# A gated cross-attention and expert kernel: the transposes of the second LayerNorm's input move from TensorE to VectorE blocks and DMAs, with four smaller edits

## The chip, the cores and the metric

The kernel runs on one core of one Trainium2 chip. Its time is the device time of one execution in microseconds; the metric is the median of the runs. Lower is better.

## What is computed

x is 2 x 1024 x 2048 in f32, the context 2 x 2048 x 2048. Cut to what matters:

```python
def fake_quant(x, scale, zp):                  # QMIN 0, QMAX 255
    q = clip(round(x / scale + zp), 0, 255)
    return (q - zp) * scale

x = x + tanh(g_xattn) * (fake_quant(layernorm(x)) @ fake_quant(ctx))
y = layernorm(x)
logits = y @ route_w.T                         # 8 experts
weight = one_hot(argmax(logits)) * max(logits)
h = einsum("bsd,erd->bser", y, A)              # 8 experts x rank 16
x = x + tanh(g_ffn) * einsum("bser,eor->bso", weight * h, Bw)
```

The first step's matmul (1024 x 2048 x 2048 for each of two batches) is the large one. In the text, "x2" is x after that first step, the input of the second LayerNorm.

## The kernel before, in words

**Tiles.** The tokens are 16 tiles of 128 rows (8 per batch). The context of a batch is 4 strips of 512 columns; a strip is loaded in 4 quarters ("st", 1 MB each), scaled to integers by ScalarE (line 347), clamped by VectorE (line 351) and kept as f16 ("q"). A tile of x is normalized and quantized by ScalarE (line 471) after statistics from VectorE (line 435) and a power on GpSimd (line 459), and is then transposed: by TensorE for tiles 0 to 3 (line 493), by a transposing DMA for the others (line 484). The product of tile t and strip s is a group of 16 matmuls into one PSUM bank (line 529, "mm").

**After a group.** VectorE adds c times the product to x in place (line 538), then adds r and corr (line 543). r is a number per row from the sum of the tile's quantized values (line 505, on ScalarE); corr is a row over all columns, from the column sums of the quantized context (line 366 for batch 0: matmuls with ones; line 377 and following for batch 1: VectorE adds first, then one matmul), both because the quantized values are kept centred on 128. Line 543 also gives the row sums of x2.

**The second step, "ffn", of a tile.** x2 is transposed by TensorE in 16 pieces of 128 x 128 ("px", line 569), ScalarE copies them to SBUF ("xnt", line 583), and 16 products with the 136 columns of A and route_w ("hl", line 576; an f32 matmul is two instructions here) follow. The mean has been taken off the weights once (line 314 and following), so hl needs x2 itself only. The variance comes from a ScalarE pass (line 601). VectorE picks the expert (lines 612 to 621), wh is transposed ("pw", line 633) and multiplied with Bw ("po", line 646, 8 instructions), and VectorE adds the result (line 654). GpSimd's queue stores the tile (line 667); the last tile is stored by SP in four pieces.

**What sets the order.** A planner at build time (class Plan) gives every task an engine, a cost, a rank, the tasks it needs and the buffers it takes. It walks through time and lets each free engine take its first ready task by rank; the instructions are then written out in that order, one stream per engine, and each engine runs its own stream strictly in order. TensorE's, ScalarE's, VectorE's, GpSimd's and SP's orders are all fixed in this way. SP issues the loads and the transposing DMAs. The planner also models DMA: a rate and a delay. Tiles are grouped into sets that share a pass over the strips: [0, 1, 2, 3], [4], [5, 6, 7], [8, 9, 10], then one by one. Buffers have fixed numbers by kind: 6 for x, 3 for st, 4 for q2 and so on; a load waits until its buffer is free. [...]

**The start.** ScalarE's queue loads six scalars, each spread to 128 partitions (line 251); SP loads x in four pieces for tile 0 (line 419), then st and x in turns.

Of the kernel before, what the change touches and what calls it, by code (L numbers as in the profile page):

```python
# [9 lines left out]
F32 = mybir.dt.float32  # L10
F16 = mybir.dt.float16
I16 = mybir.dt.int16
U8 = mybir.dt.uint8
# [30 lines left out]
class Plan:  # L44
# [4 lines left out]
    def __init__(self, units, banks, hop, dma_rate, dma_delay):  # L49
        self.units = units  # L50
        self.banks = banks
        self.hop, self.rate, self.delay = hop, dma_rate, dma_delay
        self.tasks = []
# [19 lines left out]
    def walk(self):  # L73
        free = {k: list(range(n)) for k, n in self.units.items()}
        free_banks = list(range(8))
        in_use = {k: 0 for k in self.banks}
# [12 lines left out]
        def room(t):  # L89
            want = {}  # L90
            for b in t.bufs:
                if b.unit is None:
                    want[b.kind] = want.get(b.kind, 0) + 1
            n_banks = 0
            for k, n in want.items():
                if k in self.banks:
                    n_banks += n
                    if in_use[k] + n > self.banks[k]:
                        return False
                elif len(free[k]) < n:  # L100
                    return False
            return n_banks <= len(free_banks)

        while any(waiting.values()):
            for r in [r for r in releases if r[0] <= now]:
                releases.remove(r)
                b = r[1]
                if b.kind in self.banks:
                    in_use[b.kind] -= 1
                    free_banks.append(b.unit)  # L110
                else:
                    free[b.kind].append(b.unit)
            nxt = []
            for eng, w in waiting.items():
# [19 lines left out]
                for b in pick.bufs:  # L134
                    if b.unit is None:
                        if b.kind in self.banks:
                            in_use[b.kind] += 1
                            b.unit = free_banks.pop(0)
                        else:
                            b.unit = free[b.kind].pop(0)  # L140
# [23 lines left out]
def flamingo_gated_kernel(  # L164
# [39 lines left out]
    NT = B * MT  # L204

    TURN = set(range(4, NT))
    units = {"x": 6, "st": 3, "q2": 4, "q1": 2, "q1t": 5, "xnt": 3, "wh": 2, "wht": 2, "sum": 1,
             "bn": 3, "sel": 2}
    banks = {"mm": 4, "tp": 2, "hl": 1, "po": 2, "cs": 1}
    plan = Plan(units, banks, hop=0.15, dma_rate=300e3, dma_delay=2.0)  # L210
# [9 lines left out]
    def buf(kind, name, shape, dt):  # L220
        if kind in banks:
            return Buf(kind, lambda u: psum.tile(shape, dt, tag=f"bank{u}", name=name))
        return Buf(kind, lambda u: work.tile(shape, dt, tag=f"{kind}{u}", name=name))
# [11 lines left out]
    junk = const.tile([P, D], U8, name="junk")  # L235
# [12 lines left out]

    def load_scalars():
        for i, a in enumerate((x1_scale, x1_zp, x2_scale, x2_zp, g_xattn, g_ffn)):  # L250
            nc.scalar.dma_start(raw[:, i : i + 1], a.partition_broadcast(P))

    def set_up():
        make_identity(nc, idh)
        make_identity(nc, idf)
        nc.gpsimd.memset(mhalf, -0.5)
        nc.gpsimd.memset(ones, 1.0)
        nc.gpsimd.memset(dmean, 1.0 / D)
        for e in range(E):
            nc.gpsimd.memset(order8[:, e : e + 1], float(E - e))  # L260

    def scalars():
        nc.vector.reciprocal(rs1, s1)
        nc.vector.reciprocal(rs2, s2)
# [13 lines left out]
    sets = [[0, 1, 2, 3], [4], [5, 6, 7], [8, 9, 10]] + [[t] for t in range(11, NT)]  # L278
# [5 lines left out]
    for tiles in sets:  # L284
# [10 lines left out]
    t_raw = add(ACT, 3.0, -100, load_scalars, nbytes=1)  # L295
    t_set = add(POOL, 3.0, -100, set_up)
    t_rs = add(DVE, 0.4, -50, scalars, needs=[t_raw])
    t_th = add(
        ACT, 1.5, 0.5, lambda: nc.scalar.activation(th, raw[:, 4:6], AF.Tanh), needs=[t_raw]
    )  # L300
    t_sc = add(DVE, 1.2, 0.5, gates, needs=[t_th])
    def weights(after):
# [15 lines left out]
        def subtract():  # L318
            nc.vector.tensor_tensor(
                war, war, mw.unsqueeze(1).to_broadcast([P, KC, ER + E]), ALU.subtract  # L320
            )

        a = add(PE, 4.0, 13.7, means, [t_war, t_set], [pm])
        b = add(DVE, 0.3, 13.7, lambda: nc.vector.tensor_copy(mw, pm.ap()[:, : ER + E]), [a], [pm])
        return add(DVE, 2.3, 13.7, subtract, [b]), t_wb
# [5 lines left out]
    def strip(b, s):  # L331
# [5 lines left out]
        for q in range(NQ):  # L337
            st = buf("st", f"st_{b}_{s}_{q}", [P, QK, NC], F32)
            rank = i - 4 + q * len(tiles) / NQ

            def load(q=q, st=st):
                rows = cx[b, q * QK * P : (q + 1) * QK * P, ts(s, NC)]
                nc.sync.dma_start(st.ap(), rows.rearrange("(k p) n -> p k n", p=P))

            def scale(q=q, st=st):
                part = qb.ap()[:, ts(q, QK), :]
                nc.scalar.activation(part.bitcast(I16), st.ap(), AF.Relu, bias=z2, scale=rs2)  # L347
# [5 lines left out]
            a = t_ctx[b, s, q] = add(SP, 0.6, rank, load, [], [st], nbytes=4 * P * QK * NC)  # L353
# [6 lines left out]
        if b == 0:  # L360
# [10 lines left out]
        else:  # L371
            tb = buf("sum", f"sum_{b}_{s}", [P, 4, NC], F16)

            def add_up(j):
                t, v = tb.ap(), qb.ap()
# [9 lines left out]
            for j in range(4):  # L385
# [6 lines left out]
                lambda: nc.tensor.matmul(cs.ap(), ones, tb.ap()[:, 0, :], start=True, stop=True),  # L392
# [10 lines left out]

    xb, q1t, t_x, t_q1t, t_r, rs_, t_pre, acc_sums = {}, {}, {}, {}, {}, {}, [], {}

    def tokens(t):
# [8 lines left out]
        for i in range(pieces):  # L415
            loads.append(
                add(
                    SP, 0.6, {1: -4.5, 2: -2.9, 3: -1.9}.get(t, rank - 4),
                    lambda i=i: nc.sync.dma_start(
# [6 lines left out]
        bn = buf("bn", f"bn_{t}", [P, NN, 6], F32)  # L426
        mv = small.tile([P, 2], F32, name=f"mv_{t}")
        wk = small.tile([P, 8], F32, name=f"wk_{t}")
        y, u, v, a, nb, rw, r, ve = (wk[:, i : i + 1] for i in range(8))
        mean, var = mv[:, 0:1], mv[:, 1:2]  # L430

        stats = [
            add(
                DVE, 0.68, rank,
                lambda n=n: nc.vector.bn_stats(bn.ap()[:, n, :], xx.ap()[:, ts(n, NC)]),  # L435
                [loads[n * pieces // NN]], [xx, bn],
            )
            for n in range(NN)
        ]

        def scale():
# [6 lines left out]
            nc.vector.scalar_tensor_tensor(v, mean, a, z1, ALU.mult, ALU.subtract)  # L448
            nc.vector.tensor_scalar(nb, v, -1.0, None, ALU.mult)  # L449

        
        def variance():
            nc.vector.bn_aggr(mv, bn.ap())
            nc.vector.tensor_scalar(ve, var, EPS, None, ALU.add)  # L454

        ag = add(DVE, 0.45, rank, variance, stats, [bn])
# [5 lines left out]
        qb = buf("q1", f"q1_{t}", [P, D], F16)  # L462
# [3 lines left out]
        t_q1t[t] = []  # L466
        clamps = []
        for h in range(H):
# [11 lines left out]
            clamps.append(add(DVE, 0.7 / H, rank, clamp, [d], [qb]))  # L480
        if t in TURN:
# [5 lines left out]
            t_q1t[t] = [a_] * (KC // 8)  # L487
        for h in range(0 if t in TURN else KC // 8):
            pt = buf("tp", f"pq_{t}_{h}", [P, 8, P], F16)

            def turn(h=h, pt=pt):
                for j in range(8):
                    nc.tensor.transpose(pt.ap()[:, j, :], qb.ap()[:, ts(8 * h + j, P)], idh)  # L493

            a_ = add(PE, 0.65, rank, turn, [clamps[h * H // 2], t_set], [qb, pt])
            t_q1t[t].append(
                add(
                    ACT, 1.01, rank,
                    lambda h=h, pt=pt: nc.scalar.copy(qt.ap()[:, ts(h, 8), :], pt.ap()),
# [4 lines left out]
        def row_sum():  # L504
            nc.scalar.activation(junk, qb.ap(), AF.Copy, accum_out=rw)  # L505

        d = add(ACT, 2.12, first[t] + 0.5, row_sum, clamps, [qb])
# [4 lines left out]
        acc_sums[t] = small.tile([P, NN], F32, name=f"ss_{t}")  # L512
# [5 lines left out]
    t_x2, t_mm = {}, {}  # L518

    def group(t, s):  # L520
# [5 lines left out]
        for k in range(KC):  # L526
            p = add(
                PE, 0.221, whole[t, s] + k / 100,
# [6 lines left out]
        xs = lambda: xx.ap()[:, ts(s, NC)]  # L535
        e = add(
            DVE, 0.76, i,
            lambda: nc.vector.scalar_tensor_tensor(xs(), acc.ap(), c, xs(), ALU.mult, ALU.add),  # L538
            [p, t_sc] + t_x[t], [acc, xx],
# [4 lines left out]
                xs(), xs(), rs_[t], corr[:, ts(s, NC)], ALU.add, ALU.add,  # L544
                accum_out=acc_sums[t][:, s : s + 1],
# [8 lines left out]
    def ffn(t):  # L554
        b, m = divmod(t, MT)
        end = t == NT - 1
        rank = last[t] + 1.2
        xx = xb[t]
        fs = small.tile([P, 8], F32, name=f"fs_{t}")
        nm, sq, v, r2 = (fs[:, i : i + 1] for i in range(4))  # L560
        hl = buf("hl", f"hl_{t}", [P, NC], F32)
        p = None
        for n in range(NN):
            pt = buf("tp", f"px_{t}_{n}", [P, NC], F32)
            xn = buf("xnt", f"xnt_{t}_{n}", [P, NC], F32)
# [7 lines left out]
            def product(n=n, xn=xn):  # L573
                for j in range(BPC):
                    k = n * BPC + j
                    nc.tensor.matmul(  # L576
                        hl.ap()[:, : ER + E], xn.ap()[:, ts(j, P)], war[:, k, :],
# [3 lines left out]
            a = add(PE, 0.55, rank - 0.1, turn, [t_x2[t, n], t_set], [xx, pt])  # L581
            d = add(
                ACT, 0.6, rank - 0.2, lambda pt=pt, xn=xn: nc.scalar.copy(xn.ap(), pt.ap()),  # L583
                [a], [pt, xn],
            )
            p = add(PE, 1.13, rank, product, [d, t_wc] + ([p] if p else []), [xn, hl])
# [6 lines left out]
        def inverse():  # L593
# [7 lines left out]
            lambda: nc.scalar.activation(junk, xx.ap(), AF.Square, bias=nm, accum_out=sq),  # L601
            [a], [xx],
# [3 lines left out]
        top = small.tile([P, 3], F32, name=f"top_{t}")  # L606
# [35 lines left out]
        for n in range(NN):  # L642
            po = buf("po", f"po_{t}_{n}", [P, NC], F32)
            a = add(
                PE, 0.93, rank,
# [80 lines left out]
```

## Time and profile before

| | |
|---|---|
| Median of 3 runs | 430.47 us (429.17 to 432.62) |
| The profiled execution | 428.93 us |
| Its span in the profile | 427.2 us |
| TensorE busy | 394.6 us (92%) |
| VectorE busy | 278.7 us (65%) |
| ScalarE busy | 212.6 us (50%) |
| Moved by DMA | 75.92 MB, mean 178 GB/s |
| TensorE clock granted | full in every slice |

All durations in this document come from one profiled execution. A row of the page's groups reads: line, engine, operation, out<-in with the tile names, shapes, count, then busy us and mean ns of one, then the idle time just before these instructions and what ended most of it. Matmuls overlap in the trace, so a mean ns of a matmul is longer than the time that it adds to a stream; the chain of waits, whose pieces do not overlap, shows that time. A name with q after the engine (SPq) is its sequencer, which issues DMAs.

### The profile page before, as it was taken

To read this page: it belongs to the slowest core of one execution; us is meant where nothing else is said; L and a number is where in the kernel's file an instruction comes from. 1 tells how busy PE (TensorE), PEld (TensorE's weight loads), DVE (VectorE), ACT (ScalarE), POOL (GpSimd) and SP (SyncE) were. 2 spreads that over 40 slices of the span, in tenths; PEclk is the share of its full clock that TensorE was granted. 3 is DMA by queue.
4 is the path that set the end of the run, shared out by engine and by line. 5 is a ranking of instruction groups with operands and counts; after the bars stand their busy time and mean duration, and the time that the engine had idled before them with its cause. 6 is when DMAs were issued, how large, how long until landed. Compare 5 with 4: busy or idle time off the path is not lost.

```text
span 427.2 us, 5486 instructions
## 1 busy us (share of the span) xinstructions
PE 394.6 (92%) x2100; PEld 228.9 (54%) x2100; DVE 278.7 (65%) x703; ACT 212.6 (50%) x211; POOL 22.0 (5%) x50
## 2 busy tenths in 40 slices
PE   0278999999999899999999999999999999999994
PEld 0134444447767446444765644477647474746561
DVE  2774744497555897996744899897588635354433
ACT  1699984438723457773895522368108230303030
POOL 1100000010000100100000010000101000000000
PEclk9999999999999999999999999999999999999999
DMA  4995889964016784999739654022475402010022
GB/s 130 404 351 199 290 297 359 404 236 93 2 61 235 233 265 142 335 303 394 170 96 350 257 201 114 12 38 49 139 269 136 148 2 98 2 61 38 9 91 98
DMA packets 50426, 75.92 MB, mean 178 GB/s; under 512 B 26976, under 2 KB 29024, under 8 KB 46432
## 3 DMA queue, kind: packets, MB, share of 16 engines
q1 hardware_dynamic: 47376, 59.84, 44.4%
q0 software_dynamic: 2160, 15.73, 8.9%
q8 instruction: 16, 0.26, 0.2%
q10 hardware_dynamic: 864, 0.00, 0.1%
q14 instruction: 10, 0.08, 0.1%
HBM read 52.50 MB, written 16.78 MB: 162 GB/s over the span
## 4 chain that ended last, share of the span: by engine, by line
PE 60%; issue 11%; DVE 10%; ACT 10%; DMA 7%; POOL 1%; ACTq 0%; SPq 0%; POOLq 0%
PE mm L529 40%; PE po L646 9%; PE hl L576 6%; DMA x<-in_x_dram 3%; DVE bn L435 3%; ACT q L347 3%; DMA st<-in_ctx_dram 3%; PE px L569 2%; ACT q L471 2%; PE cs L366 2%; ACT junk L601 2%; DVE x L543 1%; ACT xnt L583 1%; ACT junk L505 1%; DVE x L538 1%
## 5 line engine op out<-in xcount | busy, mean ns | idle before, releaser
L529 PE MATMUL mm<-q,q1t 128*128 128x512 f16 x1024 | 233.7, 380 | 6.7 <-DVE q L351 4.0
L529 PEld LDWEIGHTS <-q1t 128*128 128x128 f16 x1024 | 100.2, 98 | 125.2 <-issue 13.6
L347 ACT ACTIVATE q<-st,raw,rs 128x2048 int16<-128x2048 f32 x32 | 66.2, 2093 | 21.0 <-DMA st<-in_ctx_dram 18.7
L538 DVE SCALAR_TENSOR_TENSOR x<-mm,sc,x 128x512 f32<-128x512 f32 x64 | 46.5, 747 | 32.4 <-PE mm L529 32.0
L576 PE MATMUL hl<-war,xnt 128*128 128x136 f32 x512 | 65.5, 281 | 1.4 <-ACT xnt L583 1.1
L576 PEld LDWEIGHTS hl<-war,xnt 128*128 128x128 f32 x512 | 62.2, 190 | 7.1 <-ACT xnt L583 3.3
L646 PE MATMUL po<-wb,wht 128*128 128x512 f32 x128 | 61.3, 598 | 0.4 <-ACT wht L639 0.4
L654 DVE SCALAR_TENSOR_TENSOR x<-po,th,x 128x512 f32<-128x512 f32 x64 | 47.0, 748 | 21.1 <-PE po L646 19.2
L583 ACT COPY xnt<-px 128x512 f32<-128x512 f32 x64 | 35.4, 582 | 47.1 <-PE px L569 36.8
L601 ACT ACTIVATE junk<-x,fs 128x2048 uint8<-128x2048 f32 x16 | 32.1, 2004 | 39.3 <-DVE fs L589 39.1
L471 ACT ACTIVATE q<-x,wk 128x2048 int16<-128x2048 f32 (+1 forms) x17 | 33.8, 1993 | 35.3 <-DVE wk L449 35.3
L543 DVE SCALAR_TENSOR_TENSOR x<-x,wk,corr 128x512 f32<-128x512 f32 x64 | 47.3, 750 | 4.2 <-ACT corr L399 3.2
L435 DVE BATCH_NORM_STATS2 bn<-x 128x6 f32<-128x512 f32 x64 | 40.7, 682 | 10.7 <-DMA x<-in_x_dram 10.7
L569 PEld LDWEIGHTS px<-idf,x 128*128 128x128 f32 x256 | 30.3, 141 | 9.4 <-issue 4.4
L569 PE MATMUL px<-idf,x 128*128 128x128 f32 x256 | 34.7, 273 | 0.5 <-DVE x L543 0.5
L505 ACT ACTIVATE junk<-q 128x2048 uint8<-128x2048 f16 x16 | 30.6, 1912 | 8.4 <-DVE q L477 8.3
L646 PEld LDWEIGHTS po<-wb,wht 128*128 128x128 f32 x128 | 22.5, 190 | 20.1 <-issue 12.4
L351 DVE TENSOR_SCALAR q<-q 128x2048 f16<-128x2048 int16 x32 | 21.9, 689 | 16.0 <-ACT q L347 15.9
L459 POOL TENSOR_TENSOR wk<-wk,mhalf 128x1 f32<-128x1 f32 x16 | 11.9, 741 | 182.4 <-DVE wk L454 166.2
L493 PE MATMUL pq<-idh,q 128*128 128x128 f16 x64 | 5.2, 242 | 16.6 <-DVE q L477 16.5
L667 POOL DMA_DIRECT2D out_dram<-x x15 | 8.4, 560 | 200.1 <-DVE x L654 184.4
L639 ACT COPY wht<-pw 128x128 f32<-128x128 f32 x16 | 4.2, 264 | 28.4 <-PE pw L633 28.4
(62 smaller groups left out, 164.8 us busy)
## 6 DMA issues: line engine op xcount, KB each, us to landing
st<-in_ctx_dram SPq DMA_DIRECT2D x32, 1024.0 KB, 7.7
x<-in_x_dram SPq DMA_DIRECT2D x15, 1024.0 KB, 6.2
out_dram<-x POOLq DMA_DIRECT2D x15, 1024.0 KB, 4.7
war<-in_w_ar_dram SPq DMA_DIRECT2D x1, 1088.0 KB, 10.8
x<-in_x_dram SPq DMA_DIRECT2D x4, 256.0 KB, 4.8
wb<-in_w_b_dram SPq DMA_DIRECT2D x1, 1024.0 KB, 12.8
out_dram<-x SPq DMA_DIRECT2D x4, 256.0 KB, 2.4
q1t<-q SPq DMA_TRANSPOSE x12, 4.7
```

Source lines behind the costliest of these rows:

```text
L347: nc.scalar.activation(part.bitcast(I16), st.ap(), AF.Relu, bias=z2, scale=rs2)
L435: lambda n=n: nc.vector.bn_stats(bn.ap()[:, n, :], xx.ap()[:, ts(n, NC)]),
L471: nc.scalar.activation(qb.ap()[:, ts(h, hw)].bitcast(I16), xx.ap()[:, ts(h, hw)], AF.Relu, bias=nb, scale=a)
L529: lambda k=k: nc.tensor.matmul(acc.ap(), qt.ap()[:, k, :], qb.ap()[:, k, :], start=(k == 0), stop=(k == KC - 1)),
L538: lambda: nc.vector.scalar_tensor_tensor(xs(), acc.ap(), c, xs(), ALU.mult, ALU.add),
L543: lambda: nc.vector.scalar_tensor_tensor(xs(), xs(), rs_[t], corr[:, ts(s, NC)], ALU.add, ALU.add, accum_out=acc_sums[t][:, s : s + 1],),
L569: nc.tensor.transpose(pt.ap()[:, ts(j, P)], xx.ap()[:, ts(n * BPC + j, P)], idf)
L576: nc.tensor.matmul(hl.ap()[:, : ER + E], xn.ap()[:, ts(j, P)], war[:, k, :], start=(k == 0), stop=(k == KC - 1),)
L583: ACT, 0.6, rank - 0.2, lambda pt=pt, xn=xn: nc.scalar.copy(xn.ap(), pt.ap()),
L601: lambda: nc.scalar.activation(junk, xx.ap(), AF.Square, bias=nm, accum_out=sq),
L646: lambda n=n, po=po: nc.tensor.matmul(po.ap(), wht.ap(), wb[:, ts(n, NC)], start=True, stop=True),
L654: nc.vector.scalar_tensor_tensor(xs, po.ap(), gf, xs, ALU.mult, ALU.add)
```

## The change

Five edits come together.

1. **x2 of tiles 0 to 14 is transposed off TensorE.** VectorE transposes 32 x 32 blocks of x2 for each strip (four "turns" per tile, writing with a step of 16 elements), and SP issues 16 DMAs of 32 partitions x 512 elements, which move blocks to the partitions where they belong. hl then reads its weights straight from there, with a step of 16 elements. The px transposes and ScalarE copies stay for tile 15 alone. The pass for the variance now waits for the moves, since it writes its unused output over their source.
2. **The first LayerNorm's sums** of tiles 4 to 15 come from two ScalarE passes (sum, then squares around the mean) in place of four bn statistics on VectorE. For tiles 0 to 3 the statistics stay; their row sums of quantized values go to VectorE, and one of the two copies after their transposes also.
3. **r + corr is added once** over all 2048 columns, before the products, for tiles 4 to 7 and 11 to 15 (the set "late"); their step after a group is then one VectorE instruction in place of two.
4. **The six scalars** are loaded by GpSimd's queue as single packets into one row; one small matmul spreads them over the partitions. Tile 0's pieces of x are issued by SP and ScalarE in turns, and the activation table is loaded ahead.
5. **Column sums, buffers and plan.** Strips 2 and 3 of batch 0 are summed by VectorE adds and one matmul, like batch 1's. st, turned, across and xt share four "big" buffers of 1 MB; q1, sum and the last junk share three "half" ones. The sets become [8, 9], [10] in place of [8, 9, 10], and some planner costs and the DMA rate and delay are other numbers, which changes the written order on every engine.

The core of the diff:

```diff
-    units = {"x": 6, "st": 3, "q2": 4, "q1": 2, "q1t": 5, "xnt": 3, "wh": 2, "wht": 2, "sum": 1,
-             "bn": 3, "sel": 2}
-    banks = {"mm": 4, "tp": 2, "hl": 1, "po": 2, "cs": 1}
-    plan = Plan(units, banks, hop=0.15, dma_rate=300e3, dma_delay=2.0)
+    MOVE = set(range(NT - 1))
+    pools = {"x": 6, "big": 4, "q2": 4, "half": 3, "q1t": 5, "wh": 2, "wht": 2, "bn": 3, "sel": 2}
+    kinds = {k: (k, n) for k, n in pools.items()}
+    kinds |= {"st0": ("big", 4), "st1": ("big", 2), "ff": ("big", 4)}
+    kinds |= {k: ("bank", n) for k, n in (("mm", 4), ("tp", 2), ("hl", 1), ("po", 2), ("cs", 1))}
+    plan = Plan(pools | {"bank": 8}, kinds, hop=0.15, dma_rate=370e3, dma_delay=2.5)
...
-            nc.scalar.dma_start(raw[:, i : i + 1], a.partition_broadcast(P))
+            nc.gpsimd.dma_start(row[:, i : i + 1], a.unsqueeze(0))
...
-    sets = [[0, 1, 2, 3], [4], [5, 6, 7], [8, 9, 10]] + [[t] for t in range(11, NT)]
+    sets = [[0, 1, 2, 3], [4], [5, 6, 7], [8, 9]] + [[t] for t in range(10, NT)]
...
+    t_bc = add(
+        PE, 0.3, -98,
+        lambda: nc.tensor.matmul(bc.ap()[:, :6], dmean[:1, :], row, start=True, stop=True),
+        [t_raw, t_one], [bc],
+    )
...
-        if b == 0:
+        if b == 0 and s < NN // 2:
...
+            d = add(
+                ACT, 2.3, rank,
+                lambda: nc.scalar.activation(qb.ap(), xx.ap(), AF.Copy, accum_out=ssum),
+                loads, [xx, qb],
+            )
...
+            d = add(
+                ACT, 2.3, rank,
+                lambda: nc.scalar.activation(
+                    qb.ap(), xx.ap(), AF.Square, bias=nmean, accum_out=var
+                ),
+                [d], [xx, qb],
+            )
...
+    late = {t for tiles in sets if tiles[0] % MT and tiles[-1] != MT + 2 for t in tiles}
...
+        if t in late:
+            if s == 0:
+                t_added[t] = add(
+                    DVE, 2.25, i - 1,
+                    lambda: nc.vector.scalar_tensor_tensor(
+                        xx.ap(), xx.ap(), rs_[t], corr, ALU.add, ALU.add
+                    ),
+                    [t_r[t]] + t_read[t] + [t_corr[b, n] for n in range(NN)], [xx],
+                )
...
+            t_x2[t, s] = add(
+                DVE, 0.84, i,
+                lambda: nc.vector.scalar_tensor_tensor(
+                    xs(), acc.ap(), c, xs(), ALU.mult, ALU.add, accum_out=ss
+                ),
+                [p, t_sc, t_added[t]], [acc, xx],
+            )
+            return
...
+    def hidden_moved(t, xx, hl, rank):
...
+        turned = flat("ff", f"turned_{t}", F32, D)
+        across = flat("ff", f"across_{t}", F32, D)
+        turns = []
+        for n in range(NN):
+
+            def turn(n=n):
+                nc.vector.transpose(
+                    turned.ap().rearrange("p (g i k) -> p k g i", i=BLK, k=KC)[:, ts(n, BPC)],
+                    xx.ap()[:, ts(n, NC)].rearrange("p (k g j) -> p k g j", g=BPC, j=BLK),
+                )
+
+            turns.append(add(DVE, 0.6, rank - 0.5, turn, [t_x2[t, n]], [xx, turned, across]))
+        moved = []
+        for g in range(BPC):
+
+            def move(g=g):
+                for q in range(BPC):
+                    nc.sync.dma_start(
+                        across.ap()[ts(g, BLK), ts(q, NC)], turned.ap()[ts(q, BLK), ts(g, NC)]
+                    )
+
+            moved.append(add(SP, 1.8, rank - 0.5, move, turns, [turned, across], nbytes=4 * P * NC))
+        p = None
+        for h in range(NN):
+
+            def product(h=h):
+                xt = across.ap().rearrange("p (m k) -> p k m", k=KC)
+                for k in range(h * BPC, (h + 1) * BPC):
+                    nc.tensor.matmul(
+                        hl.ap()[:, : ER + E], xt[:, k], war[:, k, :],
+                        start=(k == 0), stop=(k == KC - 1),
+                    )
+
+            p = add(PE, 1.05, rank, product, moved + [t_wc] + ([p] if p else []), [across, hl])
+        return p, turned, moved
...
-            lambda: nc.scalar.activation(junk, xx.ap(), AF.Square, bias=nm, accum_out=sq),
-            [a], [xx],
+            lambda: nc.scalar.activation(junk.ap(), xx.ap(), AF.Square, bias=nm, accum_out=sq),
+            [a] + after, [xx, junk],
```

The products of tile 15 keep the old form, in a function "hidden" of the same shape as before's px, copy and product.

## The prediction

> **What bounds the kernel now.** First the busy rows, the slices and the costliest groups of the page.
>
> ```profile
> PE 394.6 (92%) x2100; PEld 228.9 (54%) x2100; DVE 278.7 (65%) x703; ACT 212.6 (50%) x211; POOL 22.0 (5%) x50
> ...
> PE   0278999999999899999999999999999999999994
> ...
> DMA  4995889964016784999739654022475402010022
> ...
> L529 PE MATMUL mm<-q,q1t 128*128 128x512 f16 x1024 | 233.7, 380 | 6.7 <-DVE q L351 4.0
> L576 PE MATMUL hl<-war,xnt 128*128 128x136 f32 x512 | 65.5, 281 | 1.4 <-ACT xnt L583 1.1
> L646 PE MATMUL po<-wb,wht 128*128 128x512 f32 x128 | 61.3, 598 | 0.4 <-ACT wht L639 0.4
> L569 PE MATMUL px<-idf,x 128*128 128x128 f32 x256 | 34.7, 273 | 0.5 <-DVE x L543 0.5
> ```
>
> TensorE is full from the fourth slice to the last but one; VectorE is at 65%, ScalarE at 50%. Its four groups wait for almost nothing. The mean ns overlap, so I take prices from the chain of waits in a late tile, where pieces follow each other:
>
> ```profile
> 344.13 0.87 PE px L569 x8
> ...
> 347.82 3.71 PE hl L576 x32
> ...
> 354.23 1.72 PE po L646 x4
> ...
> 357.88 9.07 PE mm L529 x42
> ```
>
> So px costs 0.109 us, hl 0.116, po 0.430, mm 0.216. A tile is 64 mm (13.8), 16 px (1.74), 32 hl (3.71), one pw (0.11) and 8 po (3.44): 22.8, the spacing of the px groups of two tiles (343.97 and 366.78). TensorE sets the pace. Then the start, from the timeline:
>
> ```profile
> 11.02 0.69 DVE L435 BATCH_NORM_STATS2 bn<-x 128x6 f32<-128x512 f32 x1 [3.44 <-DMA x<-in_x_dram]
> 14.28 2.37 ACT L471 ACTIVATE q<-x,wk 128x1024 int16<-128x1024 f32 x2 [3.44 <-DVE wk L449]
> 24.89 1.90 ACT L505 ACTIVATE junk<-q 128x2048 uint8<-128x2048 f16 x1
> 37.47 4.26 PE L529 MATMUL mm<-q,q1t 128*128 128x512 f16 x19
> ```
>
> Tile 0's fourth piece lands at 11.0 because its queue first waits for the scalars' transfers (the SP waits name raw); quantization starts at 14.3, ScalarE is then busy 21.0 of 21.5 us, and TensorE runs without gaps only from 37.5. Last, the two stretches in which batch 1's context is loaded:
>
> ```profile
> 127.00:180.00 53.00, 51.79 (x273) 31.20 (x272) 42.51 (x113) 30.57 (x29) 4.29 (x7) 1.00 0.74 241
> 180.00:240.00 60.00, 59.77 (x324) 35.22 (x322) 41.66 (x96) 42.53 (x37) 2.66 (x4) 1.00 0.84 268
> ```
>
> The last two columns are DMA share and GB/s: 241/0.74 and 268/0.84 give about 322 GB/s as the full rate of this mixture.
>
> [...]
>
> **The change, part by part.**
>
> *Removed from TensorE.* 15 x 16 px at 0.109: 26.2 us. Context sums of strips 2 and 3: 32 matmuls become 2, 30 x 0.216 = 6.5. All this lay on the path: -32.7.
>
> *Start.* The six scalars leave ScalarE's queue for POOL's, so tile 0's pieces no longer wait for them. POOL now issues six transfers (I take 0.6 to 1 us each from its 0.56 us output row), then the rest of its set-up, then tile 0's power. Quantization can start between 9.5 and 12 instead of 14.3; I take 11.2. From there to the last piece of strip 0 ScalarE has quantizations, scalings and two copies, 2.37 + 4 x 2.0 + 2.0 + 2 x 1.0 = 14.4 us, because row sums (2.1 each) and half of the copies (1.0) are VectorE's now or later; before it took 22.4. Counting on through tile 2 (quantize, clamp, transpose, copy), gapless work begins about 32.6, with 32 mm and 16 sums done instead of 25 and 12: 4.9 + 7 x 0.216 + 4 x 0.216 = 7.3 us. Bounds 4 and 10. VectorE's four copies (1.2) and four row sums (2.2) there, 14 us, lie in its idle time.
>
> *Tail.* The last tile keeps its old transposes; one VectorE step fewer after its last matmul, -0.7.
>
> *VectorE.* Off: 48 bn (32.7), their followers (about 7), 72 half-steps for nine tiles (54). On: 36 fused steps (27), nine full-width additions (2.35 each[...]: 21), two strips' sums (9.6), start work (14), small steps (4), and 60 turns. [...]I take 0.95[...]: 57. Sum about 317 of some 405 us, 78%[...]. *ScalarE.* 60 copies (34.9), four row sums and four half copies (12) go, 24 full-width sums of 2.2 come (52.6): 218. Both have room, so I charge their throughput nothing, and their latency below.
>
> *The moves, the new wait.* After a tile's last turn SP issues 16 transfers of 64 KB. ScalarE's queue issued its scalars every 0.48 us; 15 x 0.48 = 7.2, and the last lands some 2.4 us after issue (the 256 KB stores' median): 9.6. Bounds 8.5 and 12.5. In a late tile the chain from last matmul to hl is 0.84 + 0.95 + 9.6 and hops of 0.3: 11.7. The written order on TensorE puts 12.1, 11.5 and 12.0 us of other work there for tiles 13, 12 and 14 (56 mm; 37 mm, pw and po; 39, pw and po): covered to about 0.3. Without this cover each tile would lose 11.7.
>
> For tiles 0 to 5 it is tighter. A tile in transit holds two of the four "big" buffers, and two early quarters of batch 1 hold the rest, so tiles go one after the other: hl of one, route (1.5), four turns (3.8), moves (9.6), hl of the next: 14.9. Work between these hl in the order: 51 mm and po, 14.6; 33 mm and po, 10.7; 45 mm and po, 13.3; 14.6; 14.8 (here VectorE also has 2.2 of clamps and matmul endings in between). Missing: 0.3, 4.2, 1.6, 0.3, 2.3: 8.7 us. For the other ten tiles 0.4 each: 4. Behind the waiting moves stand context and x loads on SP, the squares on ScalarE, and hl on TensorE, which passes nothing.
>
> *DMA in the batch-1 stretch.* 127 to 240 moved 12.8 + 16.1 = 28.9 MB. With five tiles' moves it is 34.1 MB, 106 us at 322 GB/s, while TensorE's part shrinks to 113 - 10 = 103. Missing 3, and as much again for moves queued behind loads: 6.
>
> Sum on the span: 427.2 - 32.7 - 7.3 - 0.7 + 8.7 + 4 + 6 = 405.2. The median of the runs, 430.47, lies 3.3 above the profiled span: 408.
>
> **Rivals.**
>
> *All hidden.* The moves land at the cheap end and the DMA keeps up: no stalls, 405.2 - 18.7 + 3.3 = 390. For it: today TensorE shows no gap above 1.4 us after 37.5. Against: 10.7 us cannot cover 14.9.
>
> *Queue bound.* Each move set waits behind a 1 MB load (2.6 us at the 404 GB/s of the best slice) at eight tiles, 21 us: 429, about no change. For it: DMA stands at 9 in four slices of that stretch. Against: over the last 12 slices its mean is near 2.
>
> *Strided weights (slower).* hl's weights are now read with a step of 64 bytes. [...] It decides from 162 ns per load (22 us of gain / 480 + 116). Against: [...]f16 operands stream at 0.42 (216/512), so TensorE has reserve per access[...]. A gain from it is excluded.
>
> That px doesn't leave TensorE is excluded by the written order: 16 px are left.
>
> **How the numbers follow.** My forecast 0.55 (its own range 396 to 420), all hidden 0.10, queue bound 0.15, strided weights 0.20. The range 389 to 434 takes in the first three, the bounds of moves, turns and start, and the mild end of the last, and leaves some 0.17. About 1% is what a measurement of this kernel can tell from no change: below 426.2 lie 0.55 + 0.10 + half of queue bound: 0.72; between 426.2 and 434.8 0.09; above 0.19.
>
> **What would show it.** px with 16 matmuls; hl still 3.7 us per 32; [...]SP issuing moves every 0.48; gapless matmuls from about 33; TensorE waiting for the moves' landing before hl in tiles 1 to 5, longest at tile 2, and hardly after tile 10. It is wrong if hl takes over 162 ns, if moves land more than 12.5 us after the last turn, or if TensorE waits on context pieces in the batch-1 stretch for over 10 us.

## The result and the profile after

The changed kernel takes 497.0 us (median of 4 runs, 496.4 to 499.2) against 430.5 for the kernel before: 1.155 times as long, 95% interval 1.149 to 1.161. The forecast was 408, its range ended at 434. The profiled execution has a span of 495.0 us. First the page: busy time, slices and groups.

```profile
PE 416.1 (84%) x1832; PEld 251.0 (51%) x1832; DVE 310.7 (63%) x699; ACT 219.6 (44%) x188; POOL 23.6 (5%) x56
...
PE   0789999979694969695797989969997969979794
...
PEclk9999999989895989798899999998997999979799
...
L662 PE MATMUL hl<-war,across 128*128 128x136 f32 x480 | 110.1, 404 | 49.1 <-DMA across<-turned 41.0
L662 PEld LDWEIGHTS hl<-war,across 128*128 128x128 f32 x480 | 108.2, 319 | 58.4 <-issue 46.8
...
L640 DVE STREAM_TRANSPOSE turned<-x 128x512 f32<-128x512 f32 x60 | 57.4, 1034 | 1.3 <-issue 0.5
```

TensorE has 268 instructions fewer and yet is busy 21.5 us longer. One row carries that: hl, whose weights are read with a step now (110.1 us for 15 tiles; before it was 65.5 for 16). And after the eighth slice TensorE has gaps again and again, where before there were none to speak of; most of them end at hl, with the landing of a move. The clock row dips in the stretch of the gaps. The chain of waits shows one round of an early tile (pieces left out where "..." stands):

```profile
129.72 7.34 PE hl L662 x32
137.06 1.94 PE mm L585 x9
...
143.44 0.59 SPq L651
144.07 0.59 SPq L651
...
149.56 1.30 SPq L651
150.91 0.71 SPq L651
152.29 0.59 SPq L651
152.93 2.00 DMA across<-turned
155.06 7.41 PE hl L662 x32
```

hl of 32 takes 7.34 and not 3.71; from one hl to the next there are 25.3 us, more than the 22.8 that a whole tile took before. SP's own timeline gives the moves' part:

```profile
142.25 11.27 SPq L651 DMA_DIRECT2D across<-turned  x16
...
167.63 11.50 SPq L651 DMA_DIRECT2D across<-turned  x16
...
193.20 11.57 SPq L651 DMA_DIRECT2D across<-turned  x16
```

So the round is hl 7.3, route and turns 5.2 (137.06 to 142.25), issue 11.3, the last landing and a hop 1.5: 25.3. A count over 90 to 478 us (388 us): TensorE busy 333.1, idle 54.9.

### The profile page after: what moved, and what is told of

It is laid out like the page before. It is cut to its first block, busy times and chain, and to the rows that moved or that the text cites. A ratio compares the mean times of both kernels' runs of the same rounds, so it can differ in the third digit from the quotient of the medians.

```text
span 495.0 us, 5305 instructions
## 1 busy us (share of the span) xinstructions
PE 416.1 (84%) x1832; PEld 251.0 (51%) x1832; DVE 310.7 (63%) x699; ACT 219.6 (44%) x188; POOL 23.6 (5%) x56
## 4 chain that ended last, share of the span: by engine, by line
PE 44%; SPq 26%; DMA 12%; DVE 9%; issue 4%; ACT 4%; POOL 1%; DVEq 0%; ACTq 0%; POOLq 0%
SPq L651 25%; PE hl L662 18%; PE mm L585 17%; DMA across<-turned 7%; PE po L767 6%; DMA st<-in_ctx_dram 4%; DVE turned L640 3%; ACT q L362 2%; DMA row<-in_g_ffn_dram 1%; DVE x L614 1%; PE cs L384 1%; ACT q L517 1%; DVE q L369 1%; POOL row L248 1%; DVE bn L460 0%
## 5 line engine op out<-in xcount | busy, mean ns | idle before, releaser
L662 PE MATMUL hl<-war,across 128*128 128x136 f32 x480 | 110.1, 404 | 49.1 <-DMA across<-turned 41.0
L662 PEld LDWEIGHTS hl<-war,across 128*128 128x128 f32 x480 | 108.2, 319 | 58.4 <-issue 46.8
L722 ACT ACTIVATE turned<-x,mine 128x2048 f32<-128x2048 f32 x15 | 30.0, 2002 | 101.9 <-DMA across<-turned 90.8
L640 DVE STREAM_TRANSPOSE turned<-x 128x512 f32<-128x512 f32 x60 | 57.4, 1034 | 1.3 <-issue 0.5
L733 DVE TENSOR_REDUCE mine<-hl 128x1 f32<-128x8 f32 x16 | 2.7, 166 | 65.2 <-PE hl L662 62.9
L517 ACT ACTIVATE q<-x,mine 128x2048 int16<-128x2048 f32 (+1 forms) x17 | 33.7, 1990 | 16.7 <-DVE mine L501 16.6
L484 ACT ACTIVATE q<-x,mine 128x2048 f16<-128x2048 f32 x12 | 24.0, 2001 | 18.5 <-DVE mine L480 18.5
L558 ACT ACTIVATE q<-q 128x2048 f16<-128x2048 f16 x12 | 22.9, 1905 | 13.8 <-DMA q1t<-q 13.8
L475 ACT ACTIVATE q<-x 128x2048 f16<-128x2048 f32 x12 | 22.9, 1910 | 12.1 <-DMA x<-in_x_dram 11.9
L597 DVE SCALAR_TENSOR_TENSOR x<-x,mine,corr 128x2048 f32<-128x2048 f32 x9 | 21.1, 2347 | 0.2
```

Source lines behind the costliest of these rows:

```text
L517: nc.scalar.activation(qb.ap()[:, ts(h, hw)].bitcast(I16), xx.ap()[:, ts(h, hw)], AF.Relu, bias=nb, scale=a)
L640: nc.vector.transpose(turned.ap().rearrange("p (g i k) -> p k g i", i=BLK, k=KC)[:, ts(n, BPC)], xx.ap()[:, ts(n, NC)].rearrange("p (k g j ...
L662: nc.tensor.matmul(hl.ap()[:, : ER + E], xt[:, k], war[:, k, :], start=(k == 0), stop=(k == KC - 1),)
L722: lambda: nc.scalar.activation(junk.ap(), xx.ap(), AF.Square, bias=nm, accum_out=sq),
```

## The experiments

Two theories. W, strided weights: hl pays for its 64-byte step. M, the moves: 16 DMAs per tile from one queue close a round that is longer than TensorE's work. Each can be switched off by itself, at the cost of moving other values than the reference's, and then both.

**Dense weights, 16 moves.**

```diff
-                xt = across.ap().rearrange("p (m k) -> p k m", k=KC)
+                xt = across.ap().rearrange("p (k m) -> p k m", k=KC)
```

> One edit to the changed kernel: hl's weights are read densely (128 neighbouring elements per partition) and not with a step of 16 elements. Turns, moves, order and buffers stay; the output is that of another arrangement of x2, so it is no longer the reference's. Theory W (strided weights): 0.229 us per hl instruction fall back to the 0.116 of before, 32 hl take 3.7 us and not 7.3, and nearly all of 15 x 3.6 = 54 us comes off the path: 440 to 452 us. Theory M (16 moves per tile, issued in 11.5 us, close a loop hl - route - turns - moves - hl of some 25.5 us per tile, and TensorE waits in it): hl falls back too, but the loop only becomes 21.9 us, TensorE still waits for moves in batch 0, and where SP is slowed by what else it issues little is won: 455 to 482 us. If hl stays at 7.3 us per 32, the step in memory is not what makes it dear, and both fall.

Measured: 460.8 us (459.6 to 461.7), 36 below the changed kernel. That is inside M's range (15 to 42) and short of W's (54). Both are in it: TensorE's work after 90 us falls from 333.1 to 301.0, so the step was dear, and 49.0 of the 54.9 us of idle time stay. The chain of waits of this kernel shows why the work falls by 32 and not by 54:

```profile
141.56 2.54 DMA across<-turned
144.24 6.30 PE hl L662 x32
...
163.87 3.30 DMA across<-turned
167.31 6.71 PE hl L662 x32
```

After these two waits even dense weights take 6.3 to 6.7 us; after a shorter one, of 2.2 us at 123.4, they take 3.94. The windows of this kernel around the first of the two (busy times of PE, PEld, DVE, ACT and POOL, then clock, DMA share, GB/s):

```profile
141.00:144.00 3.00, 0.00 (x0) 0.00 (x0) 0.00 (x0) 0.00 (x0) 0.00 (x0) 0.71 0.74 240
144.20:147.40 3.20, 3.16 (x14) 3.19 (x15) 0.00 (x0) 1.68 (x1) 0.00 (x0) 0.50 0.83 163
```

TensorE pauses here for 5.3 us, from 139.0 to 144.2. The granted clock is 0.50 from about 142.2 to 149.1, an estimate from the means of the windows (0.71, 0.50, and 0.74 from 147.4 to 150.6). While it lasts, 14 instructions pass in 3.2 us where 28 would at the 0.116 us of before. In the changed kernel the stretches at 0.50 last 3.4 us (106.1 to 109.5, 130.0 to 133.4, 181.2 to 184.6), 6.8 (437.2 to 444.0) and 10.2 (150.5 to 160.7). The length of the pause alone does not decide: in the last two experiments an hl after a pause of 2.10 us takes 5.65, in a stretch with a mean clock of 0.94 (270 to 300), and one after a pause of 3.55 us takes 4.01. What else decides was not shown. A wait for the moves thus costs its length and, where the clock falls, up to 2.6 to 3 us more in the hl behind it (6.30 or 6.71 less 3.71).

**Strided weights, 4 moves** of 128 partitions.

```diff
-                for q in range(BPC):
-                    nc.sync.dma_start(
-                        across.ap()[ts(g, BLK), ts(q, NC)], turned.ap()[ts(q, BLK), ts(g, NC)]
-                    )
+                nc.sync.dma_start(across.ap()[:, ts(g, NC)], turned.ap()[:, ts(g, NC)])
```

> One edit to the changed kernel: 4 DMAs of 128 partitions x 2 KB per tile in place of 16 of 32 partitions x 2 KB. The bytes are the same, but the 32-row blocks stay in their partitions, so the output is no longer the reference's. Strided weights stay. Theory W: hl stays at 7.3 us per 32 and TensorE's work at that of the changed kernel, most of the loss stays: 475 to 495 us. Theory M: SP issues a tile's moves in about 2 us and not 11.5, the last one lands some 5 us after the first issue and not 13.3, the loop of a tile shrinks from 25.5 to about 17 us and TensorE's gaps of some 40 us between 90 and 300 us close: 447 to 462 us.

Measured: 443.2 us (442.1 to 445.4), on M's side and 4 below its range. SP's timeline and the chain of waits of this kernel:

```profile
134.87 2.41 SPq L650 DMA_DIRECT2D across<-turned  x4
...
152.41 2.41 SPq L650 DMA_DIRECT2D across<-turned  x4
```

```profile
101.53 6.89 PE hl L659 x32
...
122.98 6.91 PE hl L659 x32
...
231.14 7.24 PE hl L659 x32
```

The bytes are the same and the issue takes 2.4 us in place of 11.3, so it is the number of DMAs that costs: 0.60 us for each here, 0.70 to 0.72 in the changed kernel. (The blocks also stay in their partitions here; that was not tested apart.) TensorE is idle for 6.4 of 334 us (90 to 424). Without pauses the strided hl takes 6.89 per 32, 0.215 each. The hl at 231.14 follows a wait of 1.25 us, in slices with a clock of 0.9 or more, and takes 7.24, as one in the changed kernel does (at 260.15, after 0.59 us, with a clock of 1.00). So the start after a wait adds 0.35, and a clock that is 0.50 for a part of the hl 0.1 to 0.2 more (7.33 to 7.43 in the changed kernel, with means of 0.58 to 0.77).

**Both off** (dense turns too).

> Both edits to the changed kernel, hl's weights read densely and 4 DMAs per tile in place of 16, and the turns written densely (32 neighbouring elements per block) too; the output is no longer the reference's. If W and M together are the whole loss: hl 3.7 us per 32, a turn of 0.6 to 0.7 us in place of 1.03, no waits for moves worth telling, 390 to 402 us, about what the prediction called all hidden (390). If a third cost is in the change (the clock that fell to 0.94, the queue, the start): above 410 us.

Measured: 405.1 us (403.7 to 407.5), a little above the span expected. W and M, with the dense turns, are 91.9 us together; alone W and M gave 36.2 and 53.8, in all 90.0, so they about add up. A turn takes 0.687 us against 1.034 with its step; what this alone is worth was not run. Most of the 12.4 us in which TensorE is still idle (90 to 389) lie around the second batch's context:

```profile
190.00:200.00 10.00, 6.62 (x44) 4.85 (x43) 8.67 (x26) 6.75 (x5) 0.00 (x0) 0.94 0.95 318
200.00:210.00 10.00, 8.66 (x23) 3.30 (x21) 6.41 (x14) 8.25 (x9) 0.43 (x1) 0.72 1.02 289
```

From 190 to 230 it is idle for 9.2 us, while the DMA share stands at 0.95 to 1.06. TensorE's own waits there name ScalarE and VectorE, and ScalarE waited 6.0 us for pieces of the context. So at most some 9 us are the limit that the queue rival named, not 21.

**No moves; the other four edits.**

```diff
-    MOVE = set(range(NT - 1))
+    MOVE = set()
```

> One edit to the changed kernel: no tile takes the new way, x2 of all 16 tiles is transposed on TensorE as before; the other four edits (first LayerNorm's sums on ScalarE, r + corr added once, scalars as single packets, sums of two more strips on VectorE) stay. The prediction's terms for these say start -7.3, context sums -6.5, tail -0.7: 427.2 - 14.5 + 3.3 = 416 us. If ScalarE, which has 24 full-width sums more and keeps the 60 copies that the moves removed (218 + 35 = 253 us), holds TensorE up: 422 to 432. If the four edits themselves cost time and are part of the loss: above 432.

Measured: 412.3 us (411.6 to 416.0), 0.958 of the kernel before (0.955 to 0.961). TensorE is idle for 2.1 us between 90 and 398. This version beats both kernels: the four other edits together are worth 18 us, and the new way costs 85 on top of them.

**The price by step**, on the kernel with 4 moves.

```diff
-                xt = across.ap().rearrange("p (m k) -> p k m", k=KC)
+                s_ = (1, 2, 4, 8, 16)[t % 5]
+                xv = across.ap().rearrange("p (c m s) -> p c s m", s=s_, m=P)
...
-                        hl.ap()[:, : ER + E], xt[:, k], war[:, k, :],
+                        hl.ap()[:, : ER + E], xv[:, k // s_, k % s_], war[:, k, :],
```

> A price list for W, made from the kernel with 4 moves per tile (no waits before hl there): tile t reads hl's weights with a step of 1, 2, 4, 8 or 16 elements (4, 8, 16, 32, 64 bytes) in turn, so each step occurs in three tiles; the output is no longer the reference's. Known ends: 3.71 us per 32 at 4 bytes, 6.89 at 64. If the port pays[...]: 3.7 at 4 bytes, between 3.7 and 5 at 8, and the full 6.9 from 16 bytes on. If it pays for any step that is not 1: 6.9 from 8 bytes on. If the price grows with the reach: 16 and 32 bytes between 4.5 and 6. Time: three tiles of each, (0 + 0.5 + 3.2 + 3.2) x 3 = 21 us over dense by the first, so 425 to 435 us.

Measured: 433.2 us, a single run. The chain of waits, tiles 0 to 4, with steps of 4, 8, 16, 32 and 64 bytes:

```profile
101.36 3.71 PE hl L660 x32
...
119.61 3.77 PE hl L660 x32
...
134.04 7.37 PE hl L660 x32
...
154.74 7.54 PE hl L660 x32
...
176.83 6.89 PE hl L660 x32
```

The price does not grow evenly with the step: 8 bytes cost next to nothing (0.06 us per 32 instructions), 16, 32 and 64 bytes cost 3.66, 3.83 and 3.18. What in the memory makes it so was not shown. None of the five has a wait before it, and the mean clock of the run is 0.985. The later tiles repeat these values (7.36, 7.53 and 6.89 near the end).

**Strided weights without any move.** ScalarE's copies of px write xt with a step of 16 elements, and hl reads it so.

```diff
-    MOVE = set(range(NT - 1))
+    MOVE = set()
...
-                        hl.ap()[:, : ER + E], xt.ap()[:, ts(k, P)], war[:, k, :],
+                        hl.ap()[:, : ER + E], xt.ap().rearrange("p (m k) -> p k m", k=KC)[:, k], war[:, k, :],
...
-                lambda n=n, pt=pt: nc.scalar.copy(xt.ap()[:, ts(n, NC)], pt.ap()),
+                lambda n=n, pt=pt: nc.scalar.copy(
+                    xt.ap().rearrange("p (m k) -> p k m", k=KC)[:, ts(n, BPC)],
+                    pt.ap().rearrange("p (k m) -> p k m", m=P),
+                ),
```

> W alone, with no moves: the kernel without the new way (412.3 us), but ScalarE writes the transposed x2 into xt with a step of 16 elements, and hl reads its weights with that step. The values are right. W: 16 x (6.89 - 3.71) = 51 us on TensorE, which has no gaps to take it: 458 to 468 us, and hl at 6.9 us per 32. If the strided copies on ScalarE cost much more than the 0.587 us of the dense ones, TensorE waits for xt as well, and the time lies above 468. If the strided weights are dear only next to DMAs that write the same tile, hl stays at 3.7 and the time at 412 to 418.

Measured: 463.9 us (462.6 to 464.7), 51.6 above the 412.3; 16 x 3.18 is 50.9. W holds alone, with no moves at all. The chain and the groups of this kernel:

```profile
99.96 6.89 PE hl L685 x32
```

```profile
L693 ACT COPY xt<-px 128x512 f32<-128x512 f32 x64 | 60.6, 1054 | 39.8 <-PE px L679 38.6 <-PE hl L685 1.1
```

The copies cost 1.054 us here in place of 0.587, and TensorE hardly waits for them (0.2 us before hl in all): ScalarE has room for it.

**Moves on two queues.**

```diff
-                    nc.sync.dma_start(
+                    (nc.sync if g % 2 else nc.scalar).dma_start(
...
-            moved.append(add(SP, 1.8, rank - 0.5, move, turns, [turned, across], nbytes=4 * P * NC))
+            moved.append(add(SP if g % 2 else ACT, 1.8, rank - 0.5, move, turns, [turned, across], nbytes=4 * P * NC))
```

> The changed kernel, with the moves of the four target blocks alternating between SP's and ScalarE's queues: 8 of a tile's 16 DMAs each. Nothing else changes and the values are right. M by issue (SP needs 0.59 us or more for each): both queues are done in some 5 to 6 us, the last move lands 8 us after the first issue in place of 13.3, the loop of a tile falls by 5 us, and of the 54 us that four moves gave some 15 to 35 come: 460 to 482 us; ScalarE pays 8 x 0.6 = 4.8 us per tile, 72 in all, which its 44% busy time holds. M by the transfers[...]: SP's 8 issues stretch to the old 11 us, 490 to 500. If ScalarE stands waiting for the turns with quantizations behind it: above 500.

Measured: 481.2 us (480.4 to 481.4), at the weak end of M by issue. SP's timeline, then ScalarE's waits:

```profile
159.39 5.24 SPq L651 DMA_DIRECT2D across<-turned  x8
...
207.23 7.61 SPq L651 DMA_DIRECT2D across<-turned  x8
```

```profile
ACT q L558 <- DMA across<-turned: 23.1, 4, 7.6
...
ACT q L484 <- DMA across<-turned: 16.0, 1, 16.0
```

Issue is what binds: 8 DMAs on SP's queue take 5.24 to 7.61 us (135 to 246 us) where 16 took 11.3 to 11.6. But there is a new wait: the moves are issued in ScalarE's own stream, and quantizations and sums stand behind them. How much of the gain this takes was not shown.

**A step of two elements, right values.** Chunks k and k+8 lie side by side; turns and hl have a step of 8 bytes, and each move writes runs of 256 bytes.

```diff
...
-                        across.ap()[ts(g, BLK), ts(q, NC)], turned.ap()[ts(q, BLK), ts(g, NC)]
+                        across.ap().rearrange("p (c q r) -> p q c r", q=BPC, c=8)[ts(g, BLK), q],
+                        turned.ap()[ts(q, BLK), ts(g, NC)].rearrange("p (c r) -> p c r", c=8),
...
-                xt = across.ap().rearrange("p (m k) -> p k m", k=KC)
+                xt = across.ap().rearrange("p (c m s) -> p s c m", s=2, m=P)
```

> The changed kernel with another arrangement of the moved tile that keeps the values right: chunks k and k+8 lie side by side, so hl reads its weights with a step of 2 elements (8 bytes), the turns write with the same step, and each of the 16 moves writes runs of 256 bytes in place of 2 KB. W with the price list (3.77 us per 32 at 8 bytes, 7.4 at 16): hl is as cheap as dense, a turn costs 0.69 to 0.8 us, and the time is that of dense weights with 16 moves, 455 to 463 us. If the short runs cost the moves time (8 times the packets), M grows: SP's issues or the landings get longer and the time lies between 465 and 500. If SP's cadence comes from the bytes alone, no difference to 460.8.

Measured: 480.8 us (479.3 to 482.3), 20 above dense weights, in the range that was named for dearer moves. TensorE's work between 90 us and the last tile is that of dense weights (303.1 against 301.0), its idle time is not (66.9 against 49.0). The waits of this kernel:

```profile
PE hl L665 <- DMA across<-turned: 56.5, 14, 7.5
```

With dense weights it was 30.6 in 11 waits. An early set's issue is 12.0 to 12.2 us against 11.3 to 11.7, and a move lands 2.2 us after its issue against 2.0; that this and the later landings are all of the 20 us was not shown.

**Late tiles only, two queues and one.** The same, with `MOVE = set(range(10, NT - 1))`; the first with the two queues above, the second with SP's alone.

> What the causes point to, with right values: step of 2 elements as above, moves split between SP's and ScalarE's queues, and only tiles 10 to 14 take the new way, each a set of its own with 12 us of other work before its hl, at a time when SP and ScalarE have little to do. Tiles 0 to 9 and 15 are transposed on TensorE. If cover holds (0.84 + 0.7 + some 8 us of moves < 12): five times 16 px at 0.109 come off 412.3, 8.7 us: 402 to 406 us. If a tile's moves still outlast the cover by 2 us or more, the gain is spent: 410 to 418, plus up to 3 us per pause for TensorE's lower clock.

> The same with all 16 moves of a tile on SP's queue. M: SP needs about 12 us for 16, the last lands 14 after the first issue, with 1.5 before it 15.5 us against a cover of 12: five tiles each wait 3 to 4 us and run some 3 us at half clock after it, against 1.74 saved: 412 to 425 us, slower than two queues by 8 to 20. If SP is quicker in this quiet stage (0.6 us each): 9.6 + 2 + 1.5 = 13, 405 to 412.

Measured: 421.0 us (419.6 to 424.5) and 422.3 (421.1 to 424.6), 0.979 and 0.983 of the kernel before, where the version with no moves has 0.958: some 9 to 10 us above it. TensorE's timeline of the first:

```profile
351.33 9.66 PE L585 MATMUL mm<-q,q1t 128*128 128x512 f16 x44
363.55 5.61 PE L665 MATMUL hl<-war,across 128*128 128x136 f32 x32 [2.56 <-DMA across<-turned]
```

The expected gain of 8.7 did not come: where only 44 matmuls stand before hl, TensorE waits 2.6 us, and hl then takes 5.6, with the clock at 0.50 in its first half (363.55 to 366.30). The five waits are 2.10, 1.36, 0.62, 2.56 and 2.17, in all 8.8 us. After two of them (2.10 and 2.56) hl takes 5.6, after the others 4.0; that is 3.2 us more, and one wait for a copy of ScalarE, which issues half of the moves, took 2.1. Together this is 14.1 of the 17.4 us between 421.0 and the expected 403.6. With one queue four waits are 13.2 us, 2.73 to 4.07 each, but only the longest is followed by an hl of 5.65; after 3.55 us of waiting it takes 4.01. Two queues bring almost nothing over one (1.3 us, within the runs' spread), and that expectation was wrong as well. Moving these five, with 12 us of cover each, did not pay; a written order with more work before hl was not tried.

## Why the prediction was wrong, step by step

*Sum.* The span was to be 405.2 and is 495.0, 89.8 more. Two terms carry it: hl, 15 x (7.33 - 3.71) = 54.3, and idle time of 54.9 where 8.7 + 4 + 6 = 18.7 stood, 36.2 more. Together they are 90.5. Switched off one at a time, W and M were worth 36.2 and 53.8. W's gain is smaller than 54.3, because with hl dense most of the waits stay (49.0 of 54.9 us) and hl after them takes up to 6.3 or 6.7 us, at a clock of 0.50 for a part of it; M's is larger than 36.2, because four moves also take away most of the idle time that the prediction had allowed for.

*Strided weights* (the rival on the other side, 0.20). This is the step that failed first: the sum leaves hl at 3.71 us per 32 and has no term for the step in memory, which cost 54.3. The rival had the place, and the 162 ns from which it decides; no trace of before showed what such a load costs. Measured are 215 ns in a stream without pauses, 229 with them. It was set aside with "TensorE has reserve per access", from f16 operands that stream at 0.42 ns a column. Those are neighbouring elements; they say nothing on weights with a step of 64 bytes, which take 6.89 us per 32 where neighbouring ones take 3.71.

*Moves.* This is the second step that failed: the mechanism was right, the size was not. 15 x 0.48 + 2.4 gave 9.6 us; measured are 12.8 from the first issue to hl, 0.3 beyond the upper bound. From one issue to the next it is 0.63 us for most moves and up to 1.5 for some later ones, 0.72 on average. The 0.48 came from ScalarE's queue and transfers of 0.5 KB. Why the later ones are slower was not settled.

*The round of tiles 0 to 5.* Route and turns took 5.2, about as said (1.5 + 3.8). With 12.8 for the moves the round without hl is 18.0, not 14.9, against covers of 10.7 to 14.8. By the prediction's own list the missing time of tiles 1 to 5 grows by 3.1 each, to 3.4, 7.3, 4.7, 3.4 and 5.4: 24.2 us, against 8.7. TensorE's timeline of the changed kernel, with the idle time before hl in brackets:

```profile
129.72 7.34 PE L662 MATMUL hl<-war,across 128*128 128x136 f32 x32 [3.87 <-DMA across<-turned]
...
155.06 7.41 PE L662 MATMUL hl<-war,across 128*128 128x136 f32 x32 [7.34 <-DMA across<-turned]
...
180.69 7.33 PE L662 MATMUL hl<-war,across 128*128 128x136 f32 x32 [4.89 <-DMA across<-turned]
...
206.65 7.40 PE L662 MATMUL hl<-war,across 128*128 128x136 f32 x32 [4.08 <-issue]
...
233.94 7.43 PE L662 MATMUL hl<-war,across 128*128 128x136 f32 x32 [5.13 <-DMA across<-turned]
```

These are 25.3 us, longest at tile 2 as forecast. So here only the price of the moves was wrong; the round itself was described rightly. That late tiles would be covered to 0.3 fell too: one late set is issued in 12.3 us on a queue with little else (391.88 to 404.21), and hl at 405.8, 437.8 and 462.2 follows waits of 4.4, 3.3 and 3.3 us for a landing.

*What was left out.* The prediction priced each wait at its length, without the clock. In the changed kernel that was a small miss, because the strided hl is hardly slower with the clock at 0.50 for a part of it (7.33 to 7.43 against 7.24): TensorE's work after 90 us is 333.1, and 327.6 with four moves and hardly a wait, so clock and starts after waits cost about 5.5 us in all. With dense weights it is a larger one: 2.6 to 3 us for an hl of 6.3 or 6.7.

*DMA in the batch-1 stretch* was put at 6 us; with both causes off 12.4 us are idle, 9.2 of them there. *Queue bound* was wrong as the main cause: with four moves the same bytes pass and the time is 443.2.

*Start*: matmuls without gaps begin at 34.6, with exactly the 32 mm and 16 sums counted. That is 2.9 us earlier than 37.5 and 11 instructions of 0.216 ahead, 5.3 in place of 7.3, within its bounds. *VectorE* 310.7 (317 said), *ScalarE* 219.6 (218), a full-width addition 2.347 (2.35), *turn* 1.034 (0.95; both were the author's estimates, which no trace of before showed). The four other edits together were to give 416 by these steps, and 412.3 was measured; since the start gave less than said, some 6 us of this gain belong to no term of the prediction.

*All hidden* said 390: 405.1 is the nearest that was reached, with values that aren't the reference's.

## What to carry to other kernels

Taking work off the bound engine can make its remaining work dearer: check how each operand left behind is laid out (here f32 weights with a step of 8 bytes cost 0.06 us per 32 instructions, with one of 16 or more 3.2 to 3.8). Count DMAs, not bytes, when blocks are moved inside SBUF (here 0.6 to 0.7 us of one queue each, 64 KB or 256 KB), and close the round from use to use before trusting an average cover. Where a rival names a cost on the other side of the forecast and no measurement of that case contradicts it, a fast dense case is no evidence against it.

## What was not expected of the hardware

- hl's price is a step between 8 and 16 bytes, not a slope: 3.71 and 3.77 us per 32 at 4 and 8 bytes, 7.37, 7.54 and 6.89 at 16, 32 and 64. That 64 bytes is a little cheaper than 16 and 32 was seen in every tile and has no explanation here.
- Strided weights hide a halved clock: after a wait 32 take 7.24 us at a clock of 1.00 and 7.33 to 7.43 with one of 0.50 for a part of them, where dense ones take 3.94 and up to 6.7.
- After a pause of 2.10 us an hl took 5.65 us, with a mean clock of 0.94 from 270 to 300; after one of 3.55 us an hl took 4.01, in a run with a mean clock of 0.996. Stretches at 0.50 lasted 3.4, 6.8 and 10.2 us.
- A step of 64 bytes in the destination costs ScalarE's copy from PSUM 1.054 us against 0.587, and VectorE's 32 x 32 transpose 1.034 against 0.687.
